# MLP variances by a product with ones, dummy activations ahead of table switches, and a deformable product in thirds

## The chip, the cores and the metric

The kernel runs on one core of one Trainium2 chip. A core has five engines that work side by side, each with its own queue of instructions: TensorE (PE in the profile, with its weight loads as PEld), VectorE (DVE), ScalarE (ACT), GpSimd (POOL) and SyncE (SP, which issues most DMAs). They meet through semaphores. The metric is the device time of one launch in microseconds; before and after are measured in several runs each, and their medians are compared.

## What is computed

Four images of 56 x 56 positions with 128 channels, in float32. Each goes through four layers, and each layer adds its output for the group-normalised input to the image:

```python
x = x + swin(_gn(x), L0 weights)      # window attention, full attention, MLP
x = x + mamba(_gn(x), L1 weights)     # selective scan in four directions
x = x + deform_conv(_gn(x), L2 weights)
x = x + swin(_gn(x), L3 weights)

# in swin:
xf = xf + _mha(_layernorm(xf, g1, be1), ...)
h = gelu(_layernorm(xf, g2, be2) @ w1 + b1)      # 128 -> 512
xf = xf + (h @ w2 + b2)                          # 512 -> 128

def _layernorm(x, g, b, eps=1e-05):
    m = jnp.mean(x, axis=-1, keepdims=True)
    v = jnp.mean((x - m) ** 2, axis=-1, keepdims=True)
    return (x - m) * jax.lax.rsqrt(v + eps) * g + b

# in deform_conv: val is interpolated from four neighbours of a learned place, for 9 taps
out = jnp.einsum('bhwkc,kcf->bhwf', val, kernel.reshape(KK, C, F))
```

## The kernel before

The image lies in SBUF as x, 128 channels on the partitions by 3136 tokens on the free axis. Most stages walk over it in 7 chunks of 448 tokens (CH); a tile of tokens has 112 (QB), so 4 tiles make a chunk and 28 the image. The four images are worked one after the other, and for each the four layers: swin L0, mamba L1, deform L2, swin L3. Nearly all is fp32, and an fp32 matmul shows as two records.

The stages `mlp` and `deform` are written under a manual schedule: each engine gets its instructions in the order of the program text. In the attention part a scheduler may move instructions that do not depend on each other.

**MLP** (L640 to L716). The steps for chunk n are: `residual` (the attention's output product and the sum with x1, on VectorE), `center` (a product with a matrix that subtracts the mean over channels, and the square on ACT), `spread` and `ln_spread` (L149; the variance per token: four matmuls with the squares as weights put tokens on the partitions, the root on ACT and the reciprocal on VectorE over 112x4), `scale` and `ln_rows` (L162; four matmuls bring the 448 values back as rows repeated over 128 partitions, ACT copies them to SBUF, VectorE multiplies), `shift` (ACT, gain and bias), `hidden` (four products with w1 and a gelu each), `result` (four products with w2 into one bank), `store` (VectorE, and the statistics of the next group norm). Gelu and root are in different activation tables, so ACT loads a table before and after each root. The order in the loop for chunk n is center n+1, two hidden of n, spread n+1, two hidden of n, residual n+2, scale n+1, result n, shift n+1, store n. All banks come from one pool of 8. The squares (`ln_sq`), the shifted tokens (`xn2`) and the hidden values (`h`) have two buffers each.

**Group norm** (L117 to L136): statistics on VectorE, two small matmuls, then a root on ACT. Before that root ACT loads the table, if another was in use. The attention's next use of ACT is mostly exp.

**Deformable stage** (L1232 on). For each tile t: 9 gathers on GpSimd's DMA queue (L1248) bring 4 neighbours' values for each tap into a patch of four buffers; `weigh` (L1349 to L1351, VectorE) multiplies by the weights and adds up in 9 instructions; `turn` (L1362, L1363) transposes on TensorE and copies to `vt` on ACT, a copy for each third of the 9 taps. When a chunk's four tiles are turned, `product` runs 9 matmuls over 448 tokens (L1369) into the one bank `pdo`, and `add` (L1374) adds it to x and takes the statistics. The product of chunk c−1 stands after the turn of the first tile of chunk c, its add after the weighing of the second.

Of the kernel before, what the change touches and what calls it, by code (L numbers as in the profile page):

```python
# [19 lines left out]
P = 128  # L20
# [58 lines left out]
class _Net:  # L79
    def __init__(self, ctx, tc, x, packs, out):  # L80
        self.tc, self.nc, self.x_in, self.out = tc, tc.nc, x, out
        self.B = x.shape[0]
        nc = self.nc
        wp = ctx.enter_context(tc.tile_pool(name="weights", bufs=1))
        self.keep = wp
        self.w = {}
        for i, (layer, cols) in enumerate(COLS.items()):
            at, n = _offsets(cols)
            t = wp.tile([P, n], F32, tag=f"w_{layer}", name=f"w_{layer}")
            (nc.sync if i % 2 == 0 else nc.scalar).dma_start(t, packs[layer])  # L90
            self.w[layer] = {name: t[:, o : o + k] for name, (o, k) in at.items()}
        c = self.w["C"]
        self.ident, self.gmat = c["ident"], c["gmat"]
        self.ones = {1: c["ones1"], 2: c["ones2"]}
        self.center = {1: (c["center1"],), 2: (c["center2"], c["others2"])}
        self.sel = wp.tile([P, KB], F32R, tag="sel", name="sel")
        nc.vector.memset(self.sel.bitcast(F32), 0.0)
        for h in range(NH):
            nc.vector.memset(self.sel[h * DK : h * DK + 2, :].bitcast(F32), 1.0)
        self.ident2 = wp.tile([64 + NX, NX], F32R, tag="ident2", name="ident2")  # L100
        nc.vector.memset(self.ident2.bitcast(F32), 0.0)
        for k in (0, 64):
            nc.vector.tensor_copy(self.ident2[k : k + NX, :], self.ident[:NX, :NX])
        self.one32 = wp.tile([P, DK], F32, tag="one32", name="one32")
        nc.vector.memset(self.one32, 1.0)
        self.eps = wp.tile([P, 1], F32, tag="eps", name="eps")
        nc.vector.memset(self.eps, 1e-5)
        self.x = wp.tile([P, L], F32, tag="x", name="x")
        self.st = wp.tile([P, NCK, 6], F32, tag="gn_st", name="gn_st")
        self.dpool = ctx.enter_context(tc.tile_pool(name="tables", bufs=1, space=DRAM))  # L110


    def stats(self, x, c):

        self.nc.vector.bn_stats(self.st[:, c, :], x[:, c * CH : (c + 1) * CH])

    def group_norm(self, sb, ps):  # L117
        nc = self.nc
        st = self.st
        mv = sb.tile([P, 2], F32, tag="gn_mv", name="gn_mv")  # L120
        nc.vector.bn_aggr(mv, st.rearrange("p c s -> p (c s)"))
        pm = ps.tile([P, 512], F32, tag="mm", name="gn_pm")
        nc.tensor.matmul(pm[:, 0:1], lhsT=self.gmat, rhs=mv[:, 0:1], start=True, stop=True)
        mean = sb.tile([P, 1], F32, tag="gn_mean", name="gn_mean")
        nc.vector.tensor_copy(mean, pm[:, 0:1])
        dv = sb.tile([P, 1], F32, tag="gn_dv", name="gn_dv")
        nc.vector.tensor_sub(dv, mv[:, 0:1], mean)
        nc.vector.scalar_tensor_tensor(dv, dv, dv, mv[:, 1:2], ALU.mult, ALU.add)
        pv = ps.tile([P, 512], F32, tag="mm", name="gn_pv")
        nc.tensor.matmul(pv[:, 0:1], lhsT=self.gmat, rhs=dv, start=True, stop=True)  # L130
        rstd = sb.tile([P, 1], F32, tag="gn_rstd", name="gn_rstd")
        nc.scalar.activation(rstd, pv[:, 0:1], AF.Sqrt, bias=self.eps)
        nc.vector.reciprocal(rstd, rstd)
        return mean, rstd
# [27 lines left out]
    def ln_rows(self, dst, rs, bank):  # L162

        nc, k = self.nc, rs.shape[1]
        pb = bank("ln_pb")
        for i in range(k):
            nc.tensor.matmul(pb[:, i * QB : (i + 1) * QB], lhsT=rs[:, i : i + 1].to_broadcast([QB, P]), rhs=self.ident[:QB, :QB], start=True, stop=True)
        nc.scalar.copy(dst, pb[:, : k * QB])


    def swin_prepare(self, layer):
# [135 lines left out]
    def attention(self, layer, x, x1, oT, sb):  # L307
# [32 lines left out]
        with tc.manual_schedule():  # L340
# [33 lines left out]
            with tc.tile_pool(name="ap_sb", bufs=2) as tb, tc.tile_pool(name="ap_ps", bufs=8, space=PSUM) as ps:  # L374
                bank = lambda name: ps.tile([P, 512], F32, tag="mm", name=name)
                of_windows = self.windows(layer, x, x1, self.group_norm(tb, ps), tb, bank)
                nc.gpsimd.memset(kl, 0.0)
                ln = {}

# [259 lines left out]
    def mlp(self, layer, x, x1, oT, last):  # L639
# [3 lines left out]
        with tc.tile_pool(name="mlp", bufs=2) as sb, tc.tile_pool(name="mlp_ps", bufs=8, space=PSUM) as ps, tc.manual_schedule():  # L643
# [16 lines left out]
                nc.gpsimd.tensor_add(x2[:, cols(n)], x2[:, cols(n)], x[:, cols(n)])  # L660

            def spread(n):
                m["rs", n] = self.ln_spread(m["sq", n][:, 0:1, :], bank, sb)

            def scale(n):
                sq = m["sq", n]
                self.ln_rows(sq[:, 1, :], m.pop(("rs", n)), bank)
                nc.vector.tensor_mul(sq[:, 0, :], m.pop(("pc", n))[:, :CH], sq[:, 1, :])

            def shift(n):  # L670
# [25 lines left out]
            def do(f, n, *args):  # L696
                if 0 <= n < NCK:
                    f(n, *args)

            residual(0)  # L700
            for n in range(-1, NCK):
                do(center, n + 1)
                do(hidden, n, (0, 1))
                if n < 0:
                    residual(1)
                do(spread, n + 1)
                do(hidden, n, (2, 3))
                do(residual, n + 2 if n >= 0 else -1)
                do(scale, n + 1)
                do(result, n)  # L710
                do(shift, n + 1)
                do(store, n)


# [517 lines left out]
    def deform(self, b, x):  # L1232
# [7 lines left out]
        with tc.tile_pool(name="df", bufs=1) as s1, tc.tile_pool(name="df_ps", bufs=1, space=PSUM) as s1x, tc.manual_schedule():  # L1240
# [97 lines left out]
            with tc.tile_pool(name="dg", bufs=2) as sb, tc.tile_pool(name="dg_ps", bufs=2, space=PSUM) as ps:  # L1338
                turned, made = {}, {}

                def weigh(t):

                    g = patch[t].rearrange("q k (s c) -> q k s c", s=4)
                    wv = wts[2 * t // NTB][:, t % (NTB // 2) * KK : (t % (NTB // 2) + 1) * KK, :, None].to_broadcast([QB, KK, 4, P])
                    for k in range(0, KK, 3):
                        ks = slice(k, k + 3)
                        pa = ps.tile([P, 2, 512], F32, tag="pa", name="pa", bufs=1)
                        far = pa[:QB].rearrange("q a b -> q (a b)")[:, : 6 * P].rearrange("q (k s c) -> q k s c", k=3, s=2)
                        nc.vector.tensor_tensor(far, g[:, ks, 2:, :], wv[:, ks, 2:, :], ALU.mult)  # L1349
                        nc.vector.tensor_tensor(g[:, ks, :2, :], g[:, ks, :2, :], wv[:, ks, :2, :], ALU.mult)  # L1350
                        nc.vector.tensor_tensor(g[:, ks, :2, :], g[:, ks, :2, :], far, ALU.add)  # L1351

                def turn(t):
                    c, i = divmod(t, nq)
                    if i == 0:
                        turned[c] = sb.tile([P, KK, CH], F32, tag="vt", name="vt")
                    g = patch.pop(t)
                    for k in range(0, KK, 3):
                        pt = ps.tile([P, 3, QB], F32, tag="tr", name="pvt", bufs=3)
                        for m in range(3):  # L1360
                            for s in range(2):
                                nc.tensor.matmul(pt[:, m, :], lhsT=g[:, k + m, s * P : (s + 1) * P], rhs=self.ident[:QB, :QB], start=(s == 0), stop=(s == 1), is_transpose=True)  # L1362
                        nc.scalar.copy(turned[c][:, k : k + 3, i * QB : (i + 1) * QB], pt)  # L1363

                def product(c):
                    vt = turned.pop(c)
                    po = ps.tile([P, 512], F32, tag="y", name="pdo", bufs=1)
                    for k in range(KK):
                        nc.tensor.matmul(po[:, :CH], lhsT=w["kernel"][:, k * P : (k + 1) * P], rhs=vt[:, k, :], start=(k == 0), stop=(k == KK - 1))  # L1369
                    made[c] = po  # L1370

                def add(c):
                    cols = slice(c * CH, (c + 1) * CH)
                    nc.vector.scalar_tensor_tensor(x[:, cols], made.pop(c)[:, :CH], w["bias"], x[:, cols], ALU.add, ALU.add)  # L1374
                    self.stats(x, c)


                for t in range(NTB + 2):
                    c, i = divmod(t, nq)
                    if t < NTB:  # L1380
                        if t >= 4:
                            gather(t)
                        weigh(t)
                    if c >= 1 and i == 1:
                        add(c - 1)
                    if t < NTB:
                        turn(t)
                    if c >= 1 and i == 0:
                        product(c - 1)

    def finish(self, b, x, cols):

# [107 lines left out]
```

## Time and profile before

| | |
|---|---|
| median of 3 runs | 13205.76 us (13203.11 to 13208.83) |
| the profiled execution | 13430.0 us, its span 13428.2 us |
| mean TensorE clock granted in it | 0.930 |
| one MLP, from L593's last reciprocals to the last L690 | about 74 us, eight of them |
| gathers of the last deformable stage | 12180.8 to 12533.4 us |
| DVE L1374, idle before it, over all 28 | 447.6 us, of which "remote" 328.1 |

The profiled execution is 224 us longer than the median of the runs. Busy time by engine, for the stretch of one MLP (10858 to 10934 us) and of one deformable stage (12180 to 12540 us); the columns are the length, the busy time and number of instructions of each engine, the granted TensorE clock, the share of DMA and the rate:

```profile
core 0: us, PE busy (x) PEld busy (x) DVE busy (x) ACT busy (x) POOL busy (x), PEclk, DMA share, GB/s
10858.00:10934.00 76.00, 70.77 (x260) 40.52 (x252) 22.51 (x40) 48.99 (x70) 9.06 (x8) 0.93 0.00 0
12180.00:12540.00 360.00, 140.86 (x583) 98.14 (x580) 227.82 (x261) 32.91 (x78) 235.78 (x252) 0.60 0.56 161
```

In a line of the timeline the numbers are the start and the duration in us, then the engine, the line of the kernel and what it wrote from what; brackets hold the idle time of that engine just before and what ended it. In a line of the groups, after the bar, stand the busy time of all in us, the mean of one in ns and, after the second bar, the idle time before them and its releasers. The MLP's idle engines are seen in the first stretch: TensorE works 70.8 of 76 us, VectorE 22.5.

### The profile page before, as it was taken

How to read it: one execution, taken by the hardware profiler on the slowest of the kernel's cores; microseconds unless marked ns; L12 is line 12 of the kernel's file. 1: busy time of each engine (PE TensorE's matmuls, PEld its weight loads, DVE VectorE, ACT ScalarE, POOL GpSimd, SP SyncE). 2: the span in 40 equal slices, each digit the busy share in tenths (PEclk: the TensorE clock that was granted, in tenths of full speed). 3: DMA queues.
4: the chain of work that ended last, by engine and by line, in shares of the span. 5: the costliest groups of instructions: out<-in, count | busy, mean ns of one | idle time of the engine just before them, and what ended most of it. 6: DMA issues, size and time to landing. Idle time of an engine off the chain costs nothing. (4 is left out here: it accounts for less than half of the span.)

```text
span 13428.2 us, 218271 instructions
## 1 busy us (share of the span) xinstructions
PE 11694.2 (87%) x85716; PEld 7452.0 (55%) x85716; DVE 9598.0 (71%) x11883; ACT 7561.2 (56%) x19130; POOL 9947.0 (74%) x6852
## 2 busy tenths in 40 slices
PE   8989995699898999569989899956999989995699
PEld 4448883444544888344454488834445448883444
DVE  6649995665664999566556599956646659996664
ACT  5567772356556777235655677723565567762356
POOL 4949994488494999448849499943875949994397
PEclk9999996799999999679999999967999999996799
DMA  1000004200000000420000000042000000004100
GB/s 57 1 13 5 5 4 117 66 1 6 6 1 13 5 5 4 115 68 1 7 5 1 13 5 4 4 121 62 1 8 4 1 13 5 4 4 127 56 1 6
DMA packets 155651, 317.99 MB, mean 24 GB/s; under 512 B 19660, under 2 KB 89344, under 8 KB 154496
## 3 DMA queue, kind: packets, MB, share of 16 engines
q0 software_dynamic: 80640, 231.28, 6.0%
q1 hardware_dynamic: 73696, 71.21, 1.7%
q8 instruction: 678, 11.11, 0.3%
q14 instruction: 349, 2.86, 0.1%
q10 hardware_dynamic: 288, 1.53, 0.0%
HBM read 256.04 MB, written 47.90 MB: 23 GB/s over the span
## 5 line engine op out<-in xcount | busy, mean ns | idle before, releaser
L555 POOL TENSOR_TENSOR es<-es,e 128x896 f32<-128x896 f32 x2016 | 4160.6, 2090 | 131.8 <-ACT e L549 73.6
L350 DVE TENSOR_REDUCE mx<-pm 128x1 f32<-128x512 f32 (+1 forms) x4928 | 3056.8, 670 | 1406.8 <-PE pm L349 792.0
L549 ACT ACTIVATE e<-pst 128x448 f32<-128x448 f32 (+1 forms) x5600 | 2678.1, 544 | 1893.1 <-PE pst L547 1347.3
L1066 DVE TENSOR_TENSOR_SCAN hs<-da,dbu 128x928 f32<-128x928 f32 x1792 | 3632.7, 2070 | 53.5 <-ACT dbu L1059 30.9
L1075 POOL TENSOR_TENSOR hs<-hs,cb 128x896 f32<-128x896 f32 x1792 | 3473.8, 1952 | 24.6 <-ACT carry L1070 18.9
L349 PE MATMUL pm<-ks,qs 32*128 32x512 f32 (+1 forms) x9856 | 2909.3, 634 | 13.4 <-DVE nm L371 7.8
L547 PE MATMUL pst<-qs,ks 32*128 32x448 f32 x11200 | 2685.7, 548 | 0.0
L1084 PE MATMUL yt<-w_C,hs 128*116 128x128 f32 x14336 | 1865.0, 273 | 1.2 <-POOL hs L1075 1.2
L542 PE MATMUL pst<-nm,sel 32*128 32x448 f32 x5600 | 1638.6, 614 | 0.0
L1084 PEld LDWEIGHTS yt<-w_C,hs 128*116 128x116 f32 x14336 | 1570.3, 135 | 2.1 <-POOL hs L1075 2.1
L1048 PE MATMUL dbu<-dgb,ut 112*128 112x224 f32 x7168 | 1257.7, 298 | 270.0 <-DVE hs L1066 269.8
L1248 POOL DMA_INDIRECT g<-tab,idx x1008 | 942.7, 935 | 561.8 <-issue 291.0
L571 PE MATMUL po<-e,va 128*32 128x448 f32 (+1 forms) x11200 | 1352.4, 551 | 0.1
L349 PEld LDWEIGHTS pm<-ks,qs 32*128 32x128 f32 x9856 | 923.7, 185 | 745.2 <-DVE mx L350 619.7
L1048 PEld LDWEIGHTS dbu<-dgb,ut 112*128 112x128 f32 x7168 | 944.4, 192 | 535.2 <-DVE hs L1066 525.2
L1362 PE MATMUL pvt<-w_C,g 112*128 112x112 f32 x2016 | 407.0, 365 | 905.1 <-issue 664.6
L1002 ACT ACTIVATE da<-dl,A 128x112 f32<-128x112 f32 x3584 | 1194.5, 383 | 0.1
L547 PEld LDWEIGHTS pst<-qs,ks 32*128 32x128 f32 x11200 | 1098.3, 185 | 102.8 <-issue 13.7
L542 PEld LDWEIGHTS pst<-nm,sel 32*128 32x128 f32 x5600 | 570.5, 184 | 740.1 <-DVE mx L350 387.0
L1363 ACT COPY vt<-pvt 128x336 f32<-128x336 f32 x336 | 141.3, 441 | 1364.8 <-remote 695.0
L1362 PEld LDWEIGHTS pvt<-w_C,g 112*128 112x128 f32 x2016 | 319.4, 202 | 998.9 <-issue 735.5
L1070 ACT COPY carry<-hs 128x32 f32<-128x32 f32 x1792 | 398.1, 222 | 623.0 <-DVE hs L1066 614.9
(230 smaller groups left out, 15770.9 us busy)
## 6 DMA issues: line engine op xcount, KB each, us to landing
g<-tab,idx POOLq DMA_INDIRECT x1008
tab<-zero SPq DMA_DIRECT2D x4, 3364.0 KB
dl_d<-dl SPq DMA_DIRECT2D x28, 448.0 KB
dl<-dl_d SPq DMA_DIRECT2D x56, 224.0 KB
tab<-gt SPq DMA_DIRECT2D x16, 448.0 KB
out_dram<-x SPq DMA_DIRECT2D x28, 224.0 KB
tab<-gt SPq DMA_DIRECT2D x16, 336.0 KB
x<-in_x_dram SPq DMA_DIRECT2D x21, 224.0 KB
```

The lines of the kernel that those rows point to most:

```text
L349: nc.tensor.matmul(pm[:, :m], lhsT=qs[head(h), q.start : q.start + P], rhs=ks[head(h), keys], start=True, stop=True)
L350: nc.vector.tensor_reduce(mx[:, home[i][1], h, kc : kc + 1], pm[:, :m], AX.X, ALU.max)
L542: nc.tensor.matmul(t[:, :CH], lhsT=self.sel[head(h), :], rhs=nm[head(h), part(qc)], start=True, stop=False)
L547: nc.tensor.matmul(t[:, :CH], lhsT=ks[head(h), k * KB : (k + 1) * KB], rhs=qs[head(h), part(qc)], start=False, stop=True)
L549: nc.scalar.activation(e[:nk, j, :], t[:nk, :CH], AF.Exp, scale=SCALE)
L555: nc.gpsimd.tensor_tensor(s, es[g - 1, p][:nk] if k == 1 else s, e[:nk], ALU.add)
L571: nc.tensor.matmul(m["po"][head(h), :CH], lhsT=va[:nk, k, head(h)], rhs=src(h)[:nk], start=(k == 0), stop=(k == NKB - 1))
L1002: nc.scalar.activation(m["da"][:, :, n, 2:], dl(), AF.Exp, scale=A[:, j, n : n + 1])
L1048: nc.tensor.matmul(pu[:, 8 * h : 8 * h + 8, 2 + tb * TB : 2 + (tb + 1) * TB], lhsT=made[g]["ut", 2 * r + tb][:, d, :], rhs=made["r", g // ...
L1066: nc.vector.tensor_tensor_scan(flat(pairs[u // 2][:, d % 2]), flat(made[g]["da"][:, r]), flat(banks.pop(u)), 0.0, ALU.mult, ALU.add)
L1075: nc.gpsimd.tensor_tensor(hs, hs, made["r", g // 2]["cb"][:, :, r * HW : (r + 1) * HW], ALU.mult)
L1084: nc.tensor.matmul(sums[q][:YR, e * P : (e + 1) * P], lhsT=hs[:, n, :], rhs=self.ident, start=(n == 0), stop=(n == NST // 2 - 1), is_trans ...
```

## The change

Four things. In the MLP the variance comes from one product of a 128x128 matrix of ones with the squares (`ln_root`): it has the sum over channels in every partition at once, so the rows need no spreading; root and reciprocal then run over 128x448. The MLP's loop is turned: center and root run for chunk n+2, scale and shift for n+1, residual for n+4. `table_of` is a one-column activation on a constant, put at the start of every group norm (root) and behind that of the attention (exp). In the deformable stage `product` runs a third of its taps after each of the first three tiles of the next chunk, and `add` stands after the weighing of the fourth. The 32 columns of ones of the attention become a part of the matrix of ones.

```diff
--- before.py
+++ after.py
@@ -101,10 +101,12 @@
         nc.vector.memset(self.ident2.bitcast(F32), 0.0)
         for k in (0, 64):
             nc.vector.tensor_copy(self.ident2[k : k + NX, :], self.ident[:NX, :NX])
-        self.one32 = wp.tile([P, DK], F32, tag="one32", name="one32")
-        nc.vector.memset(self.one32, 1.0)
+        self.all1 = wp.tile([P, P], F32, tag="all1", name="all1")
+        nc.vector.memset(self.all1, 1.0)
+        self.one32 = self.all1[:, :DK]
         self.eps = wp.tile([P, 1], F32, tag="eps", name="eps")
         nc.vector.memset(self.eps, 1e-5)
+        self.any = wp.tile([P, 1], F32, tag="any", name="any")
         self.x = wp.tile([P, L], F32, tag="x", name="x")
         self.st = wp.tile([P, NCK, 6], F32, tag="gn_st", name="gn_st")
         self.dpool = ctx.enter_context(tc.tile_pool(name="tables", bufs=1, space=DRAM))
@@ -114,9 +116,14 @@

         self.nc.vector.bn_stats(self.st[:, c, :], x[:, c * CH : (c + 1) * CH])

+    def table_of(self, f):
+
+        self.nc.scalar.activation(self.any, self.eps, f)
+
     def group_norm(self, sb, ps):
         nc = self.nc
         st = self.st
+        self.table_of(AF.Sqrt)
         mv = sb.tile([P, 2], F32, tag="gn_mv", name="gn_mv")
         nc.vector.bn_aggr(mv, st.rearrange("p c s -> p (c s)"))
         pm = ps.tile([P, 512], F32, tag="mm", name="gn_pm")
@@ -166,6 +173,12 @@
         for i in range(k):
             nc.tensor.matmul(pb[:, i * QB : (i + 1) * QB], lhsT=rs[:, i : i + 1].to_broadcast([QB, P]), rhs=self.ident[:QB, :QB], start=True, stop=True)
         nc.scalar.copy(dst, pb[:, : k * QB])
+
+    def ln_root(self, dst, sq, bank):
+
+        pv, k = bank("ln_pv"), sq.shape[-1]
+        self.nc.tensor.matmul(pv[:, :k], lhsT=self.all1, rhs=sq, start=True, stop=True)
+        self.nc.scalar.activation(dst, pv[:, :k], AF.Sqrt, bias=self.eps, scale=1.0 / P)

 
     def swin_prepare(self, layer):
@@ -374,6 +387,7 @@
             with tc.tile_pool(name="ap_sb", bufs=2) as tb, tc.tile_pool(name="ap_ps", bufs=8, space=PSUM) as ps:
                 bank = lambda name: ps.tile([P, 512], F32, tag="mm", name=name)
                 of_windows = self.windows(layer, x, x1, self.group_norm(tb, ps), tb, bank)
+                self.table_of(AF.Exp)
                 nc.gpsimd.memset(kl, 0.0)
                 ln = {}

@@ -660,11 +674,12 @@
                 nc.gpsimd.tensor_add(x2[:, cols(n)], x2[:, cols(n)], x[:, cols(n)])

             def spread(n):
-                m["rs", n] = self.ln_spread(m["sq", n][:, 0:1, :], bank, sb)
+                sq = m["sq", n]
+                self.ln_root(sq[:, 1, :], sq[:, 0, :], bank)
+                nc.vector.reciprocal(sq[:, 1, :], sq[:, 1, :])

             def scale(n):
                 sq = m["sq", n]
-                self.ln_rows(sq[:, 1, :], m.pop(("rs", n)), bank)
                 nc.vector.tensor_mul(sq[:, 0, :], m.pop(("pc", n))[:, :CH], sq[:, 1, :])

             def shift(n):
@@ -698,17 +713,19 @@
                     f(n, *args)

             residual(0)
+            residual(1)
+            center(0)
+            residual(2)
+            spread(0)
             for n in range(-1, NCK):
-                do(center, n + 1)
                 do(hidden, n, (0, 1))
-                if n < 0:
-                    residual(1)
-                do(spread, n + 1)
+                do(scale, n + 1)
+                do(center, n + 2)
                 do(hidden, n, (2, 3))
-                do(residual, n + 2 if n >= 0 else -1)
-                do(scale, n + 1)
+                do(shift, n + 1)
+                do(residual, n + 4)
+                do(spread, n + 2)
                 do(result, n)
-                do(shift, n + 1)
                 do(store, n)

 
@@ -1362,12 +1379,12 @@
                                 nc.tensor.matmul(pt[:, m, :], lhsT=g[:, k + m, s * P : (s + 1) * P], rhs=self.ident[:QB, :QB], start=(s == 0), stop=(s == 1), is_transpose=True)
                         nc.scalar.copy(turned[c][:, k : k + 3, i * QB : (i + 1) * QB], pt)

-                def product(c):
-                    vt = turned.pop(c)
-                    po = ps.tile([P, 512], F32, tag="y", name="pdo", bufs=1)
-                    for k in range(KK):
-                        nc.tensor.matmul(po[:, :CH], lhsT=w["kernel"][:, k * P : (k + 1) * P], rhs=vt[:, k, :], start=(k == 0), stop=(k == KK - 1))
-                    made[c] = po
+                def product(c, i):
+
+                    if i == 0:
+                        made[c] = ps.tile([P, 512], F32, tag="y", name="pdo", bufs=1)
+                    for k in range(3 * i, 3 * i + 3):
+                        nc.tensor.matmul(made[c][:, :CH], lhsT=w["kernel"][:, k * P : (k + 1) * P], rhs=turned[c][:, k, :], start=(k == 0), stop=(k == KK - 1))

                 def add(c):
                     cols = slice(c * CH, (c + 1) * CH)
@@ -1375,18 +1392,19 @@
                     self.stats(x, c)

 
-                for t in range(NTB + 2):
+                for t in range(NTB):
                     c, i = divmod(t, nq)
-                    if t < NTB:
-                        if t >= 4:
-                            gather(t)
-                        weigh(t)
-                    if c >= 1 and i == 1:
+                    if t >= 4:
+                        gather(t)
+                    weigh(t)
+                    if c >= 1 and i == 3:
                         add(c - 1)
-                    if t < NTB:
-                        turn(t)
-                    if c >= 1 and i == 0:
-                        product(c - 1)
+                    turn(t)
+                    if c >= 1 and i < 3:
+                        product(c - 1, i)
+                for i in range(3):
+                    product(NCK - 1, i)
+                add(NCK - 1)

     def finish(self, b, x, cols):
```

## The prediction

> **What bounds the kernel now.** I read the page first (span, busy shares, slices, chain of waits), then the table of instruction groups, then the timelines of one MLP and one deformable stage.
>
> ```profile
> span 13428.2 us, 218271 instructions
> PE 11694.2 (87%) x85716; PEld 7452.0 (55%) x85716; DVE 9598.0 (71%) x11883; ACT 7561.2 (56%) x19130; POOL 9947.0 (74%) x6852
> PE 15%; DVE 4%; POOL 2%; ACT 2%; issue 1%; another core or an unknown queue 1%; DMA 0%; SPq 0%; DVEq 0%; POOLq 0%; ACTq 0%
> ```
>
> No engine is full over the whole span, so each stage has its own limit; the chain of waits could be followed over only a quarter of the span and decides little. The change touches eight MLPs, four deformable stages and the table loads at the group norms. The order of all other instructions on the engines is the same in both built programs, so only these three are priced.
>
> MLP: TensorE in a steady stretch of the MLP of batch 3, layer L0 (start, duration, then what ran; an fp32 product is two passes, so x2 is one product):
>
> ```profile
> 10881.19 0.92 PE L147 MATMUL ln_pc<-x,w_C 128*128 128x448 f32 x2
> 10881.94 1.67 PE L679 MATMUL ph<-xn,w_L 128*128 128x448 f32 x4
> 10883.44 0.86 PE L156 MATMUL ln_pv<-w_C,ln_sq 128*112 128x1 f32 x8
> 10884.16 1.75 PE L679 MATMUL ph<-xn,w_L 128*128 128x448 f32 x4
> 10885.75 0.92 PE L653 MATMUL py<-oTi,w_L 128*128 128x448 f32 x2
> 10886.50 1.04 PE L167 MATMUL ln_pb<-w_C,ln_rs 112*128 112x112 f32 x8
> 10887.38 3.19 PE L686 MATMUL py<-h,w_L 128*128 128x448 f32 x8
> 10890.40 0.92 PE L147 MATMUL ln_pc<-x,w_C 128*128 128x448 f32 x2
> ```
>
> Each line begins where the one before ends: TensorE sets the period, 10890.40 − 10881.19 = 9.21 us per chunk. A 128x448 product takes 0.75 us by the differences of starts (10881.94 − 10881.19, and 2.99/4 for the four after 10887.38; 0.747 in the mean). The variance takes 10884.16 − 10883.44 = 0.72, the spreading of the rows 10887.38 − 10886.50 = 0.88.
>
> Deformable stage: the gathers on GpSimd, and one wait of VectorE.
>
> ```profile
> 12245.53 0.93 POOL L1248 DMA_INDIRECT g<-tab,idx  x1 [0.30 <-issue]
> 12246.77 0.93 POOL L1248 DMA_INDIRECT g<-tab,idx  x1 [0.30 <-issue]
> ...
> 12295.07 0.68 DVE L1374 SCALAR_TENSOR_TENSOR x<-pdo,w_L,x 128x448 f32<-128x448 f32 x1 [34.26 <-remote]
> ```
>
> Gathers start 1.24 us apart; 252 per batch make 312 us, 11.2 us per tile of tokens, against 9 × 0.955 = 8.6 us of VectorE weighing per tile. So POOL bounds this stage, unless the 34 us waits count.
>
> The durations that the sum needs:
>
> ```profile
> L593 DVE RECIPROCAL rest<-rest 128x112 f32<-128x112 f32 x224 | 181.9, 830 | 0.5
> L272 DVE RECIPROCAL m<-m 128x16 f32<-128x16 f32 x64 | 16.2, 253 | 2.2
> L159 DVE RECIPROCAL ln_rs<-ln_rs 112x4 f32<-112x4 f32 x140 | 24.9, 178 | 367.0 <-ACT ln_rs L158 367.0
> L680 ACT ACTIVATE h<-ph,w_L 128x448 f32<-128x448 f32 x224 | 137.3, 633 | 32.2 <-PE ph L679 18.2
> L168 ACT COPY ln_sq<-ln_pb 128x448 f32<-128x448 f32 x112 | 59.6, 533 | 127.1 <-PE ln_pb L167 127.1
> L132 ACT ACT_TABLE_LOAD x8 | 10.3, 1283 | 56.4 <-PE gn_pv L130 56.4
> ```
>
> **What the Trainium skill says.** (1) "ScalarE: Activation LUTs", section "What ACT_TABLE_LOAD costs": a load takes about 1283 ns, and every switch about 2.66 us with a drain. The trace agrees with 1283, not with the drain: in this MLP a load starts at 10884.30 and the square root at 10885.59, so a switch costs 1.29 us; I use 1.29. The same section prices an activation with a pointer bias at 280 + 0.833·N ns, 653 for 448 columns; the gelu row above shows 633, which I use for the new square root. (2) "VectorE: DVE Perf Modes", section "Walkthrough: the 8-slice pipeline in each mode", has the reciprocal as an iterative divide with a repeat count of 8, so it costs several cycles per element. The trace agrees: the three rows above lie on 154 ns + 6.04 ns per element. (3) "Trace Analysis", section "DMA Instruction — SWDGE (GPSIMD)": the recorded end of such an instruction is the end of descriptor making, not of the transfer. So 1.24 us is GpSimd's own pace, and no row shows the gather landing.
>
> **The change, part by part.**
>
> *MLP.* Per chunk it removes four variance products (0.72), four row products (0.88) and the copy to SBUF (ACT, 0.53), and adds one product with ones (0.75), a square root over 128x448 instead of 112x4 (0.63 for 0.26) and a reciprocal over 128x448 instead of 112x4. That reciprocal isn't in the trace: by the line above it is 0.154 + 448 × 0.00604 = 2.86 us; four pieces of 830 ns would be 3.3. Bounds: 2.8 from the slope alone, 3.9 if every element took eight cycles of the 1.05 ns that VectorE's plain operations take per element here (an estimate from 625 ns for 448, and the skill's eight). I take 2.86.
> New sums per full chunk: TensorE 11 × 0.747 = 8.22 (was 9.07 of work, and 0.14 of gaps); ACT 2 × 1.28 + 0.63 + 0.54 + 4 × 0.63 + 0.76 = 7.0; VectorE 2.86 + 0.68 + 0.69 + 0.63 + 0.62 = 5.5. All under 9.21.
> The loop is also turned: centre and root are computed for chunk n+2, the residual for n+4. VectorE's order per chunk is scale, residual sum, reciprocal, store, statistics; ACT's is two gelus, square, two gelus, shift, load, root, load. The new wait is the store of chunk n, now queued behind the reciprocal, and behind it the next scale, the next shift, the next load and root. That makes a loop of root to reciprocal 2.86, store 0.69, statistics 0.63, scale 0.62, shift 0.76, load 1.28, root 0.63: 7.47, and about 0.4 for the handing over (0.07 to 0.1 at each of five changes of engine in this trace): 7.9 us. It lies just under TensorE's 8.22, and binds only in the two chunks that have no residual left, where TensorE needs 7.47: about 1 us per MLP. Of the eight PSUM banks, taken in turn, that of the ones product is waited for longest: it needs the store of the chunk before, which ends about 1.9 us before TensorE gets there.
> Start: now the first hidden product is at 10870.86, 8.7 us after the first residual sum at 10862.16, with row products, two loads and five hand-overs in that stretch. In the new order it is sum, centre, square, load, ones, root, reciprocal 2.86, scale, shift: 0.6 + 0.1 + 0.9 + 0.6 + 0.75 + 0.75 + 2.86 + 0.65 + 0.8 with gaps: 8.1 to 8.7. I call it equal.
> From 10870.86 on, 69 products are left (28 hidden, 28 result, 5 centre, 5 ones, 3 residual): 51.5 us, ending at 10922.4; now the last result ends at 10933.4. That is 11.0, less 1 for the loop: 10 us per MLP, 80 us in eight. What does not depend on the removal of gaps is 9.07 − 8.22 = 0.85 per chunk, 6.0 per MLP, 48 in all: the lower bound.
> In L3 the statistics wait for the next batch's tokens to arrive by DMA, as before: from store to statistics 5.2 us in this trace, against 8.2 per chunk. No cost.
>
> *Tables.* The empty activations are meant to fetch the tables before ACT has to wait. They depend on nothing but a constant, and the built program has those of the later group norms moved forward into the attention's start; the eight loads at the group norm's root are still behind the wait for gn_pv. Total loads 364 for 365. What is added is an exp and a sqrt load, about 3 us, after each attention's root: beside the reciprocal and three normalisations of tokens (0.775 each) and a product on the other engines, about 3.5 us. Nothing; without that cover 8 × 1 = +8; if all L132 loads had gone, −8 × 1.28 = −10.
>
> *Deformable products.* Nine products after the first tile of the next chunk (6.7 to 8 us in one block of TensorE) become three after each of three tiles, and the sum on VectorE moves from behind the second tile's weighing to behind the fourth's. No work is saved. If POOL runs at 1.24 us per gather, VectorE has 11.2 − 8.6 = 2.6 us spare in each tile and the sum waits at no cost: gain 0. But in the profiled execution the gathers took 352.6 us per batch (12180.8 to 12533.4), 40 over 312, of which 23 is the first wait for the table; and it is 13430.0 − 13205.8 = 224 us longer than the plain runs, 56 per deformable stage if it lies there. I take the stalls (TensorE and ACT idle with "issue" and "remote" as releaser, which the profile can't explain) as of profiling. Bounds: 0 to −30 per batch (the 29.5 us that gathers waited on "remote").
>
> Sum: MLP −80, tables 0, products 0. Against the profiled execution 13430.0 − 80 = 13350; against the median 13205.76 − 80 = **13125 us**. 0.2% is 26 us, about what this measurement can tell from no change.
>
> **The rivals.**
> - *B, the stalls of the deformable stages are real in plain runs, and the spreading takes away part*: 34 us waits speak for it; the excess of 224 us in the profiled run against. −80, and 15 to 30 per batch: about 13035.
> - *C, MLP gains only TensorE's own work*: the loop of 7.9 us is close to 8.22, and 0.3 more at the start or end eats the gaps: −48, 13158.
> - *D, no change*: the loop through ACT and VectorE is 1.3 us longer than I sum it, or the reciprocal takes 4.2: period 9.2 again, 13206.
> - *E, slower, by the reciprocal*: over 448 columns it stands in the loop of every chunk, and store, scale and shift queue behind it. From 4.2 us on the loop is longer than 9.21; 0.54 us more (4.7) already makes +26 over 48 periods. At 12.4 ns per element, twice the slope, it takes 5.7 us, the period is 10.75 and the MLPs lose 1.5 × 48 = 74: 13280. Against it: three rows on one line, so a long reciprocal has no reason to be dearer per element.
> - *The tables don't do what they say*: taken as given above.
>
> **How the numbers follow.** Mine 0.50 (13100 to 13150), B 0.17, C 0.16, D 0.09, E 0.08. Range 13040 to 13200: it holds mine, C, most of B and part of D. Faster by over 0.2% (under 13179): mine, B, and C but for a little: 0.81. Within 0.2%: D and that little: 0.11. Slower: E: 0.08.
>
> **What would show it.** Right: TensorE's starts in the MLP 8.2 us apart with lines that touch; the reciprocal at 2.8 to 2.9 us; 64 to 65 us from the reciprocals before an MLP to its last store, where it is 74; 364 table loads; gathers still 1.24 us apart. Wrong: gaps on TensorE before the hidden product with ACT's xn as releaser (C to E, by their size); a reciprocal over 4 us (E); gathers that take 320 us instead of 353 (B).

## The result, and the profile after

| | before | after |
|---|---|---|
| median of 4 runs each | 13204.44 us (13196.25 to 13208.83) | 13123.10 us (13095.61 to 13126.99) |
| ratio, with its 95% interval | | 0.9935 [0.9917, 0.9952] |
| the profiled execution, its span | 13428.2 us | 13093.7 us |
| an MLP, from the first of the last four L593 (now L607) reciprocals to the end of the last store, eight of them | 73.7 to 78.2, in all 610 us | 66.0 to 66.3, in all 530 us |
| gathers of one deformable stage, first to last start | 351.0 to 353.9 us | 310.6 to 310.9 us |

The change makes the kernel 81 us faster; 13125 was forecast. Note the third row: the two profiled executions lie 335 us apart, four times what the runs say. Read from the two traces alone, the deformable stages would seem to bring most of it: from first gather to last add the four of them take 1541 us before and 1308 after, 234 of the 335. That is the trap of this case, and the experiments take it apart.

The page of the kernel after (span, busy shares, chain of waits):

```profile
span 13093.7 us, 216642 instructions
PE 11654.7 (89%) x84932; PEld 7362.6 (56%) x84932; DVE 9728.0 (74%) x11883; ACT 7560.0 (58%) x19097; POOL 9942.8 (76%) x6852
PE 16%; DVE 5%; ACT 2%; issue 1%; POOL 1%; DMA 0%; DVEq 0%; ACTq 0%; SPq 0%; POOLq 0%
```

TensorE has 784 matmul records less (seven fewer products of two passes for each of 56 chunks) and is busy 40 us less; VectorE is busy 130 us more, mostly for the long reciprocals. The shares say nothing of where time was won. The timeline of TensorE in the same MLP as before does (start, duration, what ran):

```profile
10622.63 1.67 PE L694 MATMUL ph<-xn,w_L 128*128 128x448 f32 x4
10624.14 0.92 PE L154 MATMUL ln_pc<-x,w_C 128*128 128x448 f32 x2
10624.89 1.67 PE L694 MATMUL ph<-xn,w_L 128*128 128x448 f32 x4
10626.39 0.92 PE L667 MATMUL py<-oTi,w_L 128*128 128x448 f32 x2
10627.14 0.92 PE L180 MATMUL ln_pv<-ln_sq,all 128*128 128x448 f32 x2
10627.89 3.17 PE L701 MATMUL py<-h,w_L 128*128 128x448 f32 x8
10630.90 1.67 PE L694 MATMUL ph<-xn,w_L 128*128 128x448 f32 x4
```

A chunk now takes 10630.90 − 10622.63 = 8.27 us (9.21 before), and every line begins where the one before ends, as in the timeline of before: TensorE still sets the period. The variance costs one line, L180, of 0.75. The timeline of VectorE, in two later chunks without a residual:

```profile
10646.39 2.95 DVE L679 RECIPROCAL ln_sq<-ln_sq 128x448 f32<-128x448 f32 x1 [3.63 <-ACT ln_sq L181]
10649.25 0.59 DVE L705 SCALAR_TENSOR_TENSOR x<-py,w_L,x 128x448 f32<-128x448 f32 x1
10649.88 0.63 DVE L117 BATCH_NORM_STATS2 gn_st<-x 128x6 f32<-128x448 f32 x1
10650.42 0.61 DVE L683 TENSOR_TENSOR ln_sq<-ln_pc,ln_sq 128x448 f32<-128x448 f32 x1
10653.90 2.95 DVE L679 RECIPROCAL ln_sq<-ln_sq 128x448 f32<-128x448 f32 x1 [2.88 <-ACT ln_sq L181]
```

Here is the loop that the prediction named: reciprocal, store, statistics, scale, then shift, load and root on ACT, then the next reciprocal, 10653.90 − 10646.39 = 7.51 us. TensorE has 7.52 of work in such a chunk. The distance from one turn to the next is the period, whoever sets it; that the loop itself is about as long shows in its having no slack: on VectorE each step follows at once, and on ACT the shift starts at 10651.18, the load at 10651.94 and the root at 10653.24, with at most 0.15 us between any step and the next. The table loads, first a line of the groups, then what the view of one line tells of the group norm's root (L139; the last row is the engine's idle time before it in us, and how often):

```profile
L121 ACT ACT_TABLE_LOAD x16 | 20.5, 1283 | 1.9 <-PEq L1510 1.7
```

```profile
L139 ACT ACT_TABLE_LOAD  x8: 1283/1283/1283, 10.3 to 10670.0; - x8
...
  PE gn_pv L137: 148.0, 16
```

The root still has its eight loads, and ACT still waits 148 us for gn_pv there (151.5 before). The dummies have 16 loads of their own, and others went away: 364 in all, 365 before.

### The profile page after: what moved, and what is told of

The parts are those of the page before. It is cut to its first block, busy times and chain, and to the rows that moved or that the text cites. A ratio compares the mean times of both kernels' runs of the same rounds, so it can differ in the third digit from the quotient of the medians.

```text
span 13093.7 us, 216642 instructions
## 1 busy us (share of the span) xinstructions
PE 11654.7 (89%) x84932; PEld 7362.6 (56%) x84932; DVE 9728.0 (74%) x11883; ACT 7560.0 (58%) x19097; POOL 9942.8 (76%) x6852
## 5 line engine op out<-in xcount | busy, mean ns | idle before, releaser
L1379 PE MATMUL pvt<-w_C,g 112*128 112x112 f32 x2016 | 366.7, 338 | 623.4 <-issue 520.4
L288 POOL TENSOR_TENSOR pz<-s,m 64x784 f32<-64x784 f32 x128 | 191.8, 1498 | 751.9 <-DVE m L285 520.0
```

## The experiments

The experiments were measured in four sets, each on one chip with the unchanged kernel beside it. That mattered: the unchanged kernel had medians of 13407.7, 13406.5 and 13406.5 us on three chips and 13190.0 on a fourth; the runs in the result's table and in the table ahead of the prediction, 13204 and 13206, belong with the fourth. I call them long and short chips. Each chip served one set only, so the chip and the time of measuring aren't told apart. All but the last experiment ran on long ones.

### Is it the profiling, or the chip?

The kernel before, unchanged:

> The kernel before, unchanged, a second time: what the comparison itself tells apart, ratio 1.000 within 0.1%. Its profiled execution again at about 13430 us with gathers of 350 us per batch if profiling makes the stalls; about 13200 with 311 if the first one was a chance.

Measured: 13414.43 us, ratio 1.0004 [0.9995, 1.0012] on a long chip, profiled execution 13417.3, gathers of 351 to 355 us. Here the run whose trace is shown is no longer than the others. The timeline of this trace shows what the stalls are (TensorE, then ACT):

```profile
12257.98 1.89 PE L1362 MATMUL pvt<-w_C,g 112*128 112x112 f32 x18
12282.84 7.27 PE L1362 MATMUL pvt<-w_C,g 112*128 112x112 f32 x42 [22.97 <-ACT vt L1363]
...
12282.35 0.44 ACT L1363 COPY vt<-pvt 128x336 f32<-128x336 f32 x1 [29.81 <-remote]
```

The transposes have ended at 12259.9, but ACT's copy of them begins 22 us later, and the trace names nothing that it could have waited for ("remote" stands for another core or a queue that the profile doesn't tell); TensorE then waits for that copy. Copies ahead of which ACT idles over 5 us in this way come 15 to 18 times in each deformable stage of this trace, and the kernel after has them too:

> The changed kernel, unchanged, beside before on the chip that this set gets. If the deformable stalls belong to some chips and not to profiling: where before runs at about 13400, ratio near 0.9918 (the 66 us of the MLP alone and the 43 of the thirds alone, 110 in all) and gathers of 350 us per batch in the profile; where before runs at about 13204, ratio 0.9935 and 311 us. If the thirds take the stalls away: gathers of 311 us on either.

Measured: 13283.49 us, ratio 0.9904 [0.9889, 0.9919] on a long chip, gathers of 351 to 354 us. The thirds don't take the stalls away. In the profile of the kernel after on a short chip, and in that of the last experiment, there is none: the same kernel, profiled both times, has gathers of 311 us on one chip and 351 to 354 on another, so profiling alone doesn't make the stalls. Of the 191 us between the spans of these two traces, 183 lie between the first gather and the last add of the deformable stages. What makes a chip long stays open.

### The MLP part alone

```diff
-                m["rs", n] = self.ln_spread(m["sq", n][:, 0:1, :], bank, sb)
+                sq = m["sq", n]
+                self.ln_root(sq[:, 1, :], sq[:, 0, :], bank)
+                nc.vector.reciprocal(sq[:, 1, :], sq[:, 1, :])
...
-                self.ln_rows(sq[:, 1, :], m.pop(("rs", n)), bank)
...
             for n in range(-1, NCK):
-                do(center, n + 1)
                 do(hidden, n, (0, 1))
+                do(scale, n + 1)
+                do(center, n + 2)
...
```

> The kernel before with the MLP part of the change alone (ones product, root and reciprocal over 448 columns, turned loop). Theory (the MLP carries all): 80 us less than before, ratio 0.994, each MLP about 66 us instead of 74 to 78. Rival (the thirds of the deformable product carry part also in plain runs): only 40 to 60 less. In its profiled execution the theory that the deformable stalls come from profiling together with the block of nine products has the gathers at 350 us per batch; if the stalls of before were a chance of one execution, 311.

Measured: 13341.15 us, ratio 0.9953 [0.9939, 0.9966], so 46 to 82 us less, 66 in the middle. MLPs of 66.1 to 67.6 us, 84 less in all than in the trace of before on the same chip, and gathers still of 353 to 354. Traces don't price the part to better than 20 us: the trace with the dummies alone, on the same chip and with the same MLPs as before, has MLPs that are 17 us shorter in all than that of before. Why is seen under the turned loop below. Outside the MLPs, some places got longer: the three attentions of L0 that follow an MLP take 2 to 7 us more than before. (The four of L3 take some 11 us less together, so whether anything is lost on balance isn't shown.) The same four products of the attention's first part, in before and in this kernel:

```profile
3511.24 1.03 PE L349 MATMUL pm<-ks,qs 32*128 32x448 f32 x8
```

```profile
3491.19 1.88 PE L356 MATMUL pm<-ks,qs 32*128 32x448 f32 x8
```

They took 1.88 instead of 1.03: the clock granted from 3490 to 3499 us was 0.62 here, and 1.00 in the same place of before (3510 to 3519). The work is the same, and what made the clock drop here wasn't tested.

### Product and turned loop apart

First the upper part of that diff without the loop:

> Before with the ones product, root and reciprocal over 448 columns, but the old order of the loop (root for chunk n+1 in the same turn that scales and shifts it). Theory: TensorE has less work but must wait for root, reciprocal 2.95, scale and shift one after the other: period 8.8 to 9.2 us per chunk, 5 to 40 us less than before in all, ratio 0.997 to 1.000, and a gap on TensorE before the first hidden product of each chunk with ACT's xn as releaser. Rival (the order doesn't matter): as the MLP part alone, 0.995 and MLPs of 66 us.

Measured: 13398.10 us, ratio 0.9995 [0.9987, 1.0003]; MLPs of 75.3 to 77.0 us. TensorE's timeline in it:

```profile
10858.49 0.95 PE L148 MATMUL ln_pc<-x,w_C 128*128 128x448 f32 x2
10859.75 1.77 PE L687 MATMUL ph<-xn,w_L 128*128 128x448 f32 x4 [0.31 <-ACT xn L680]
...
10867.74 0.96 PE L148 MATMUL ln_pc<-x,w_C 128*128 128x448 f32 x2
10869.00 1.77 PE L687 MATMUL ph<-xn,w_L 128*128 128x448 f32 x4 [0.30 <-ACT xn L680]
```

The period is 9.25: TensorE has its 8.2 us of work and waits for the rest, before the first hidden product (for xn) and within the result. Less work on the engine that sets the period brought nothing: the chain from root over the reciprocal, scale and shift to the next hidden product took its place.

The other half is the lower part of the diff, the turned loop with the old variance:

> Before with the turned loop but the old variance products, rows and copy. Theory: TensorE's work per chunk stays at 9.07, only the gaps go (0.14 per chunk and some at the start): MLPs of 71 to 75 us, 10 to 30 us less than before in all, ratio 0.9977 to 0.9993. Rival (the turning carries the gain): 0.995, MLPs of 66 us.

Measured: 13369.93 us, ratio 0.9970 [0.9960, 0.9981]; MLPs of 68.9 to 72.1 us, shorter than expected. The steady period stays at 9.21, and what is won lies at the ends. From the first hidden product of a chunk to that of the next it is 8.46, 8.46 and 6.91 us at the end of an MLP, where before has 9.21, 9.21 and 8.32: the last chunks have no residual, centre or variance left, and the first ones have them while TensorE waits anyway. That is 2.9 us per MLP, 23 in all. About as much lies in the first chunk, and there it is the clock. The first chunk of the second MLP, from its first hidden product to that of the next chunk, in before on a long chip, in this kernel and in the MLP part alone (the granted clock is the third number from the end):

```profile
3300.07:3313.58 13.51, 13.51 (x36) 7.76 (x37) 1.96 (x4) 8.33 (x11) 0.65 (x1) 0.68 0.00 0
```

```profile
3294.29:3303.59 9.30, 9.30 (x39) 5.57 (x39) 1.70 (x5) 8.42 (x12) 1.14 (x1) 1.00 0.00 0
```

```profile
3289.36:3299.42 10.06, 10.06 (x22) 5.01 (x23) 5.30 (x4) 8.46 (x11) 1.13 (x1) 0.83 0.00 0
```

The five traces with the old MLP have first chunks of 9.4 us at a granted clock of 1.00, of about 11 at 0.84 or 0.85 and of 13.4 to 13.9 at 0.66 to 0.69, mixed within one trace. This is most of what makes their eight MLPs take 596, 600, 610, 616 or 617 us in all, for the full chunks after the first take 9.21 in each. With the turned loop and the old variance, seven of eight first chunks take 9.3 at 1.00; with the product too they take 9.8 to 11.4 at 0.73 to 0.86. Why the clock stays higher there wasn't tested.

By the medians 37 us (25 to 54 by the interval) come of the turned loop, and the rest of the MLP part's 66 only of the product and the loop together; the two were measured on different chips.

### The price of the reciprocal in the loop

```diff
+ spare = sb.tile([P, CH], F32, tag="spare", name="spare", bufs=1)
+ nc.vector.reciprocal(spare[:, :CH], sq[:, 1, :CH])
  nc.vector.reciprocal(sq[:, 1, :], sq[:, 1, :])
```

> The changed kernel with a second reciprocal over 448 columns into a spare tile ahead of the one that counts: 2.95 us more in the loop of root, reciprocal, store, scale, shift. Theory (that loop is 7.5 us, just under TensorE's 8.27): it becomes 10.4 and sets the period; with the start MLPs of 78 to 86 us, 110 to 160 more than the changed kernel, so slower than before where before has MLPs of 75 to 78. Rival (VectorE's idle time hides it): MLPs of 66 to 69 us.

Measured: 13400.89 us, ratio to before 0.9994 [0.9985, 1.0002]; MLPs of 78.5 to 84.6 us, 15.7 more than in the changed kernel in the mean, 117 us in all by the medians. The loop in VectorE's timeline:

```profile
10863.84 2.95 DVE L680 RECIPROCAL spare<-ln_sq 128x448 f32<-128x448 f32 x1 [2.19 <-ACT ln_sq L181]
10866.83 2.95 DVE L681 RECIPROCAL ln_sq<-ln_sq 128x448 f32<-128x448 f32 x1
...
10874.24 2.95 DVE L680 RECIPROCAL spare<-ln_sq 128x448 f32<-128x448 f32 x1 [2.18 <-ACT ln_sq L181]
```

10.40 us from one to the next, 7.51 + 2.95 to within 0.1: the loop now sets the period. These lines are of layer L0. In L3, where the statistics stand elsewhere in VectorE's order or are missing, it is 10.09, and 9.75 in the last MLP. And the loop doesn't set it from the start: the first two distances between reciprocals are 8.0 and 9.4 us in every MLP. In all this kernel comes out level with before, because the deformable part of the change is still in it. With a quarter of the reciprocal (112 columns instead of CH):

> The changed kernel with an extra reciprocal of 112 columns (0.83 us) into a spare tile ahead of the one that counts. Theory (the loop of 7.5 us has 0.75 to spare against TensorE's 8.27 and none in the two or three chunks of 7.52): 1.7 to 3.7 us more per MLP, MLPs of 68 to 70 us, 13 to 30 us more than the changed kernel, ratio to before 0.991 to 0.993 where before runs at 13400. Rival (time is lost in every chunk as the loop grows): 0.83 x 7 = 5.8 per MLP, 46 us, ratio 0.994.

Measured: 13293.19 us, ratio 0.9918 [0.9905, 0.9932], 10 more than the changed kernel on another long chip, a little less than expected; MLPs of 66.9 to 69.6, mean 68.5, 2.1 more, as expected. TensorE's full chunks stay at 8.27: the 0.83 us hide in them. The start is 0.9 longer in all eight MLPs. The two chunks without a residual keep their 7.52, other than expected, and in L0 the last distance grows from 6.01 to 6.97. Six of the eight first chunks are 1 us longer, at a clock of 0.73 to 0.76.

### The deformable product

The thirds alone:

```diff
-                    if c >= 1 and i == 1:
+                    if c >= 1 and i == 3:
                         add(c - 1)
...
-                    if c >= 1 and i == 0:
-                        product(c - 1)
+                    if c >= 1 and i < 3:
+                        product(c - 1, i)
```

> The kernel before with the deformable product in thirds alone. Theory: no change in plain runs, within 0.1% (ratio 0.999 to 1.001), since GpSimd's gathers at 1.24 us set this stage; profiled execution near 13200 instead of 13430, gathers 311 us per batch. Rival (stalls are real in plain runs): 60 to 120 us less, ratio 0.991 to 0.995.

Measured: 13364.43 us, ratio 0.9964 [0.9950, 0.9977] on a long chip. There is a gain, as the rival had it, but mostly a smaller one: 43 us by the medians, 31 to 67 by the interval, where it put 60 to 120. Gathers still take 350 to 356 us. What is shorter is the end: the last weighing comes 6 to 9 us behind the last gather, and 18 to 24 in before. VectorE at the end of the last stage of before, on this chip (weighing, add of the last chunk but one, weighing):

```profile
12507.07 0.95 DVE L1351 TENSOR_TENSOR g<-g,pa 112x768 f32<-112x768 f32 x1
12526.76 0.68 DVE L1374 SCALAR_TENSOR_TENSOR x<-pdo,w_L,x 128x448 f32<-128x448 f32 x1 [18.74 <-remote]
...
12528.02 0.95 DVE L1349 TENSOR_TENSOR pa<-g,wt 112x768 f32<-112x768 f32 x1
```

The add waits 18.7 us, and the weighing of two tiles is queued behind it. In the four stages of this trace the add at this place waits 13.4 to 18.7 us. In two of them the trace names its product as what ended the wait; here the product had ended at 12509.4, and for the 17 us after that the trace names no cause, as with the stalls above. So either the thirds or the later add could be the cause:

```diff
-                for t in range(NTB + 2):
+                for t in range(NTB + 4):
...
-                    if c >= 1 and i == 1:
+                    if c >= 1 and i == 3:
                         add(c - 1)
```

> Before with the deformable product still in one block of nine after the next chunk's first tile, but its add on VectorE moved from behind the weighing of the second tile to behind that of the fourth. On a chip where before runs at 13400, theory (an add that waits for a late product holds up the weighings queued behind it; the later place frees them): 30 to 60 us less, ratio 0.9955 to 0.998, last weighing 6 to 14 us behind the last gather instead of 18 to 24. Rival (the thirds carry it, by giving TensorE back to the transposes): ratio 0.999 to 1.001. On a chip with 13204 both expect no change.

Measured: 13346.31 us, ratio 0.9961 [0.9948, 0.9975], last weighing 6.2 us behind the last gather. The later add alone does it; the thirds aren't needed. The add of the last chunk but one now stands behind the last weighing and waits for nothing in all four stages. What the add (L1374 in both) waited for, over all 28, in before and in this kernel, both on long chips:

```profile
  remote: 274.9, 11
  PE pdo L1369: 128.7, 14
  PE pvt L1362: 36.9, 2
  issue: 14.1, 1
```

```profile
  remote: 75.5, 7
  PE pdo L1369: 36.5, 4
  issue: 1.5, 1
```

455 us of waiting became 114. This sum doesn't price the gain: with the thirds, whose add has the same later place, it is still 357, and the time is about the same. What counts is the one wait ahead of the last weighings. In the kernel after on a short chip there are four waits, one in each stage, at the last add:

```profile
  PE pdo L1387: 31.9, 4
```

### Dummy activations alone

```diff
+        self.table_of(AF.Sqrt)
         mv = sb.tile([P, 2], F32, tag="gn_mv", name="gn_mv")
...
+                self.table_of(AF.Exp)
                 nc.gpsimd.memset(kl, 0.0)
```

> The kernel before with the dummy activations alone. Theory (moved forward by the scheduler, loads still behind the group norm's wait): within 0.1% of before, and 8 loads still at the group norm's root. Rival: 10 us less if the loads were hidden, 8 more if the added loads stood on the path; both under what 0.1% tells.

Measured: 13410.34 us, ratio 1.0001 [0.9993, 1.0009]. No effect, and the eight loads stay.

### Two more kernels

The same product of ones in the attention's layernorm, on top of the change:

```diff
-                    ln[c] += (self.ln_spread(ln[c][1][:, 0:1, :], bank, tb),)
+                    sq = ln[c][1]
+                    self.ln_root(sq[:, 1, :], sq[:, 0, :], bank)
+                    nc.vector.reciprocal(sq[:, 1, :], sq[:, 1, :])
...
-                    self.ln_rows(sq[:, 1, :], rs, bank)
```

> The changed kernel with the attention's layernorm by the product with ones as well: per chunk one product instead of eight small ones, root and reciprocal over 448 columns, no copy. Theory (TensorE isn't what the attention's first part waits for; VectorE gets 2.8 us more per chunk there, 56 chunks, 157 us of work): 0 to 40 us more than the changed kernel, ratio to before 0.991 to 0.994 where before runs at 13400. Rival (the copy and rows were on the path): 20 to 60 us less, ratio 0.986 to 0.989.

Measured: 13460.12 us, ratio 1.0039 [1.0025, 1.0053], 177 us more than the changed kernel on another long chip, far outside what was expected. The group of the new reciprocals:

```profile
L403 DVE RECIPROCAL ln_sq<-ln_sq 128x448 f32<-128x448 f32 x56 | 165.4, 2953 | 71.4 <-ACT ln_sq L181 71.4
```

165 us of VectorE work for some 10 of small reciprocals, and about as much is lost: from the third on, the chunks of the attention's first part are 3 to 4 us further apart, 20 to 24 us for an attention. The same stretch of the second image's L0, in the changed kernel on a long chip and in this one (after the length, the busy time of TensorE, its weight loads, VectorE, ACT and GpSimd):

```profile
3348.80:3502.60 153.80, 136.48 (x975) 90.90 (x974) 89.72 (x166) 89.00 (x168) 37.45 (x34) 0.94 0.00 1
```

```profile
3390.70:3564.20 173.50, 144.27 (x877) 91.62 (x876) 107.22 (x165) 89.89 (x161) 37.33 (x34) 0.87 0.00 1
```

VectorE was busy 58% of it, which looked like room; but it is 17.5 us busier now, and the stretch is 19.7 longer. Two things are mixed in that. TensorE idles 12 us more, as it would if the chain of waits passed through VectorE. It is also busy 8 us longer for less work, under a clock of 0.87 instead of 0.94. How the loss divides wasn't tested.

The MLP part, one block of nine products and the later add, without dummies:

> Before with the MLP part of the change, the deformable product in one block of nine, and its add behind the weighing of the fourth tile; no dummy activations. Where before runs at 13400: the two parts alone gave 66 and 60 us, so 125 less, ratio 0.9906, last weighing 6 us behind the last gather, the same as the changed kernel (0.9904). Rival (the thirds bring something of their own): ratio 0.993 or more. Where before runs at 13204: 0.9935.

Measured: 13103.27 us, before 13190.04 on this (short) chip, ratio 0.9938 [0.9925, 0.9952]; gathers of 310.6 to 310.9 us. The same as the changed kernel within the intervals. So on a short chip neither thirds nor dummies are missed; the combination wasn't run on a long one.

## Why the prediction was right, point by point

- *TensorE's period in the MLP*: 8.22 forecast, 8.27 measured, with lines that touch. Right.
- *Reciprocal*: 2.86 taken from three shorter rows, 2.95 measured. The line through them holds up to 448 columns to within 3%.
- *The loop*: 7.9 forecast, 7.51 measured. The steps without handing over summed to 7.47, so the term of 0.4 for that was too much: store and scale begin 0.1 us before the record of the step ahead of them ends, which pays for the changes of engine. The forecast took off 1 us per MLP for this loop; that cost isn't there, for it is only TensorE's equal in the chunks without a residual. The doubled reciprocal, 10.40 us with a second one that took 2.99 from start to start, puts the loop at 7.41.
- *What is left after the first hidden product*: 51.5 us forecast. It began at 10612.71 and the last result's line (10663.22 and 3.17) ends at 10666.4: 53.7. Some 1.65 of it is the first chunk: its first four passes take from 10612.71 to 10615.86, 3.15 us, where later ones take 1.50, with a granted clock of 0.57, after a wait of 3.0 us for xn. The term was sized without that. The trace of before has the same slow start, 3.14 us for these passes from 10870.86 on, so taking a sum at full clock from the measured end of before made the gain 2 us too large.
- *Start*: called equal; from the first residual sum to the first hidden product it is 8.7 us before and 8.8 after.
- *Sum for the MLPs*: −80; 610 − 530 = 80 by the two traces. It came out partly by luck: the MLP that was worked through gained 8.7, not 10, and takes 66.2 us, not 64 to 65; others, of 76 to 78 us before, gained up to 12. Those have the first chunks at a clock below 0.7, of which the forecast had nothing: it multiplied one MLP by eight. With the five traces of the old MLP in the place of before, the difference is 65 to 87 us. Alone on a long chip the part gave 66 [46, 82].
- *Tables*: no effect, loads still behind the wait for gn_pv. Right.
- *Deformable products, forecast 0*: here a step was wrong, though it didn't move the forecast. "I take the stalls … as of profiling" doesn't hold: they belong to some chips, whose plain runs have them too. The first trace of before has the gathers of a long chip and its plain runs the times of a short one, which is what made it look like profiling. Rival B had this right for the long chips. That 13125 met the result is luck in this: the result, too, was measured where before takes 13204; on a long chip the same change gave 123 us by the medians, of which 80 were forecast. There the part gave 43 us, 8 to 17 per stage by the interval, where rival B put 15 to 30, and not by fewer stalls, as B has it, but by the add that no longer stands ahead of the last weighings.
- How the 81 us of the short chips divide wasn't measured there: before has no trace from one, and neither part ran alone on one. The changed MLPs take the same on both kinds (530 and 531 us in all), so an estimate from the traces above gives them 65 to 87 us, which leaves little for the later add. That the thirds and the dummies add nothing clear of the interval there is what the last experiment shows.
- *Rival E*: its mechanism was shown by the doubled reciprocal, its price was put too high. With 5.9 us of reciprocals the eight MLPs take 657 us, 40 to 61 more than in the five traces of the old MLP, where 74 was worked out for 5.7. The sum had a period of 10.75 forty-eight times; the trace has 10.40 in L0 and 10.09 or 9.75 in L3, and shorter distances at the start of each MLP. The turned order also has cheaper ends than the old one, which the sum left out.

## What to carry to other kernels

Taking work off the engine that sets a loop's period pays only if the loop of waits through the other engines is shorter than the new period: here the product of ones was worth nothing in the old order, and the turned order is what let it count. The same replacement in the attention cost 177 us, though VectorE was busy only 58% of the stretch: a low busy share doesn't say that work can be added there for nothing. Before comparing two traces, look at the granted clock at the same place of both. Before a trace's stalls are put down to profiling, profile the same kernel on more than one chip, and put an add that waits for another engine behind the work that doesn't need it.

## What was not expected of the hardware

- Chips of the same kind differ by 1.6% on the same kernel (13407 against 13190 to 13204 us), each as measured in one set. In the two traces of the changed kernel nearly all of it lies in one kind of stage: 351 to 354 us of gathers against 311. ACT begins copies late there, one 22 us after the products it copies, with no releaser in the trace.
- The granted TensorE clock falls to 0.62 for about 9 us at a place of the attention where it was 1.00 before, and products of 1.03 us take 1.88 there.
- The first chunk of an MLP, the same work each time, took 9.4 us at a granted clock of 1.00 and 13.5 at 0.68 within one execution of the kernel before; over eight MLPs this moved the sum between 596 and 617 us from trace to trace.
